# Second layer: where a rounding, an addition and a reciprocal stand among the work of ScalarE and VectorE

## The chip, the cores and the metric

The kernel runs on one core of a Trainium2 chip. TensorE (PE) multiplies matrices, VectorE (DVE) and ScalarE (ACT) do the elementwise work, GpSimd (POOL) a few small powers, and SyncE (SP) starts nearly all the DMAs. Each engine works through its own list of instructions in order and waits for the others through semaphores. The metric is the device time in microseconds (us) of one execution, as the median of several runs.

## The reference

Two layers work on x of shape (4, 512, 256), in float32. Each one normalizes x, computes a mixing branch s and a gated feed-forward branch, and adds their product to x:

```python
x = L0_attn_x
xn = _layernorm(x, axis=-1)
s = _L0_attn_ref(xn, ...)
g = _silu(_L0_ffn_ref(xn, ...))
x = x + s * g
xn = _layernorm(x, axis=-1)
s = _L1_attn_ref(xn, ...)
g = _silu(_L1_ffn_ref(xn, ...))
x = x + s * g
```

The feed-forward branch computes `silu(x @ W1.T) * (x @ W3.T)` with 1024 hidden values, a Walsh-Hadamard transform over them, and a product with W2. The second layer's mixing branch is a causal softmax attention over 512 positions with a second layer norm ahead of it:

```python
scores = jnp.where(causal[None], q @ k.T * scale, -jnp.inf)   # per batch
out = jax.nn.softmax(scores) @ v @ o_proj + residual
```

## The kernel before, in words

The four batches are worked on one after another, first all of layer one, then all of layer two. All products are made from pairs: a value is split into a high half that has been rounded to TensorE's fast format (`split`, line 59: ScalarE rounds, VectorE subtracts) and a low half, and a product is the sum of three matmuls, high by high, high by low and low by high.

In layer two the function `ffn_s` (line 556) handles one batch's feed-forward branch in four steps q = 0 to 3, each with a quarter of the hidden values. The up-projections of a step are done by a Strassen-like scheme of seven products in three PSUM banks: `gate_` (gu…g), `lin` (gu…l) and `z` (gu…z). The order is A11 into `gate_`, S1 into `z`, S2 into `gate_`, S4 into `z`, S3 into `gate_`, A12 into `lin`, A22 into `gate_`. Between them VectorE and ScalarE copy what the banks hold so far: `lin` from `gate_` (line 629), `h1` from `z` (635), `v` from `gate_` (638), then v = z + v (647) and h1 = gate_ + h1 (650). In q = 1 VectorE makes these copies, in other steps ScalarE. Each copy has to be done before TensorE accumulates on in that bank. At the end Silu is applied to h1 and h0 (599), and they are multiplied by v (654) and by `lin` (668), and split (hh and hl, lines 61 and 62). In the trace the tile h carries both h1 and h0.

The attention of the same batch and the down-projection (`behind`) of the step before are laid between these products at eight places per step, through the lists `places`. The order of TensorE's instructions is fixed by hand this way (`line["fixed"]`). The order on VectorE and ScalarE is chosen by the scheduler of the language, unless an `issue_after` (the helper `after`, line 458) puts an instruction behind another. Names that the steps speak of:

- `sc` (line 795): scores of a tile of 128 rows, with mask (812) and row maximum (814), for the tiles 0 to 3.
- `soft` (818): the exponentials (829) of two tiles, each with its sum in `den`. They need another activation table than Silu has, so a table load stands ahead of the first, and another ahead of the next Silu. `first["table"]` keeps the instruction behind which the next one with a table has to stand.
- `pt` (836): transposes of the exponentials on TensorE, then a split of them (ph, pl).
- `pv` (850): product with v; `rden` is the reciprocal of the sums (854), by which line 867 scales the product and adds it to xn.
- `left` in `ffn_s`: the split of h0 of step q = 0 is done in step q = 1, behind the copy of v.
- `gate` (685): for the batch before, g = silu(feed-forward) (692), times s (698), added to x (699), and the store of that half (1039); it is called for half 0 and half 1 by `later_gates` in step q = 1. In batch 0 this was done earlier, for layer one, so no such addition stands there.
- `xt` and `tq`: the next batch's transposed input and its product with the joint query and key weights, in steps 2 and 3.

SP starts, in order, the loads of the next step's weights (`load_s`, line 344), the small round trip through DRAM that spreads the second norm's moments (`there`, `mrb`), and the stores of finished halves.

Of the kernel before, what the change touches and what calls it, by code (L numbers as in the profile page):

```python
# [21 lines left out]
P = 128  # L22
# [13 lines left out]
def kernel(ctx: ExitStack, tc: tile.TileContext, a: dict, out: bass.AP):  # L36
# [7 lines left out]
    def t4(name, shape, dt=F32):  # L44
        return act.tile(shape, dt, tag="t4", name=name, bufs=10)
# [510 lines left out]
    def ffn_s(name, b, pairs, w2, beside, before, last=None):  # L556

        w2h, w2l = w2  # L560
        xh, xl = xTs[1, b]
        outs, dns = {}, []

        def out_of(t):
            if last is not None:
                if t not in outs:
                    outs[t] = psum(f"{name}dn{t}", [P, D], **DN[t // 2])
            elif t not in outs:
                dns.append(psum(f"{name}dn{t // 2}", [P, 2, D], tag="dn", bufs=2))
                outs[t], outs[t + 1] = dns[-1][:, 0, :], dns[-1][:, 1, :]  # L570
            return outs[t]

        def down(q, c, hs, tiles):
            for t in tiles:
                hh, hl = (h[:, c, sl(t % 2)] for h in hs[t // 2])
                o = out_of(t)
                for n, (l, r) in enumerate(((hh, w2h), (hh, w2l), (hl, w2h))):
                    matmul(
                        o, l, r[:, 2 * q + c, :],
                        start=q + c + n == 0 and (t % 2 == 0 or last is not None),  # L580
                        stop=q == NH // 2 - 1 and c == 1 and n == 2,
                        skip_group_check=True,
                    )

        def units(q, hs):

            return [
                lambda c=c, tiles=tiles: down(q, c, hs, tiles) for tiles in ((0, 1), (2, 3)) for c in range(2)
            ]

        def bank(n):
            return psum(f"{name}gu{n}", [P, 2, D], tag="gu", bufs=3)

        def halves(n, dt=F32):
            return hid(f"{name}{n}", dt).rearrange("p (c n) -> p c n", c=2)

        def silu(o, i):
            with after(first["table"]):
                first["table"] = nc.scalar.activation(o, i, AF.Silu)

        hidden, behind, left = {}, before, []
        for q in range(NH // 2):
            wh, wl = pairs(q)
            places = beside[q]

            def place(n):
                for what in places[n]:
                    if isinstance(what, tuple):
                        down(what[0], what[1], hidden[what[0]], what[2])
                    elif isinstance(what, int):  # L610
                        behind[what]()
                    else:
                        what()

            def product(o, i, j, begin=False, end=False):


                for n, (w, x) in enumerate([(wh, xh), (wl, xh), (wh, xl)]):
                    for c in range(2):
                        matmul(  # L620
                            o[:, c, :], w[:, i, sl(c)], x[j],
                            start=begin and n + c == 0, stop=end and n == 2, skip_group_check=True,
                        )

            copy = nc.vector.tensor_copy if q == 1 else nc.scalar.copy
            gate_ = bank(f"{q}g")
            product(gate_, A11, B11, begin=True)
            lin = bank(f"{q}l")
            copy(lin, gate_)
            place(0)  # L630
            place(1)
            z = bank(f"{q}z")
            product(z, S1, T1, begin=True)
            h1, v, h0 = halves(f"h1_{q}"), halves(f"v{q}"), halves(f"h0_{q}")
            copy(h1, z)
            place(2)
            product(gate_, S2, T2)
            copied = copy(v, gate_)
            for what in left:
                with after(copied), after(first["table"]):  # L640
                    what()
            left = []
            place(3)
            product(z, S4, B22, end=True)

            with after(first.pop("scaled", None)):
                nc.vector.tensor_tensor(v, z, v, ALU.add)
            place(4)
            product(gate_, S3, T3)
            nc.vector.tensor_tensor(h1, gate_, h1, ALU.add)  # L650
            place(5)
            product(lin, A12, B21, end=True)
            silu(h1, h1)
            nc.vector.tensor_tensor(h1, h1, v, ALU.mult)
            hs = [(halves(f"hh{i}_{q}", F32R), halves(f"hl{i}_{q}", F32R)) for i in range(2)]
            split(h1, *hs[0])
            place(6)
            product(gate_, A22, T4, end=True)
            hidden[q] = hs
            if last is not None and q == NH // 2 - 1:  # L660

                for c in range(2):
                    silu(h0[:, c, :], gate_[:, c, :])
                    nc.vector.tensor_tensor(h0[:, c, :], h0[:, c, :], lin[:, c, :], ALU.mult)
                    split(h0[:, c, :], *(z[:, c, :] for z in hs[1]))
                break
            silu(h0, gate_)
            first["gate"] = nc.vector.tensor_tensor(h0, h0, lin, ALU.mult)

            left.append(run(split, h0, *hs[1]))  # L670
            if q:
                left.pop()()
            place(7)
            behind = units(q, hs)
        if last is None:
            return behind, dns
        for q, c, t in (
            (2, 0, 2), (2, 1, 2), (2, 0, 3), (2, 1, 3), (3, 0, 0), (3, 1, 0), (3, 0, 1), (3, 1, 1),
            (3, 0, 2), (3, 0, 3), (3, 1, 2), (3, 1, 3),
        ):  # L680
            down(q, c, hidden[q], (t,))
            if (q, c) == (3, 1):
                last(t, outs[t])

    def gate(name, dn, s, x, store=None, halves=range(2)):

        rest = []
        for i in halves:
            ts_ = slice(2 * i, 2 * i + 2)
            g = t2(f"{name}g{i}", [P, 2, D])  # L690
            with after(first["table"]):
                first["table"] = nc.scalar.activation(g, dn[i], AF.Silu)
            rest.append((g, ts_))

        def add():
            for i, (g, ts_) in zip(halves, rest):
                with after(first.get("moments")):
                    nc.vector.tensor_tensor(g, g, s[:, ts_, :], ALU.mult)
                nc.vector.tensor_tensor(x[:, ts_, :], x[:, ts_, :], g, ALU.add)
                if store is not None:  # L700
                    store(i, ts_)

        return add
# [27 lines left out]
    class Attention:  # L731
# [83 lines left out]
                    self.neg[:, t : t + 1], self.scs[t][:, : (t + 1) * P], AX.X, negate=True  # L815
                )

        def soft(self, h):

            b, ins = self.b, first["table"]  # L820
            if h == 0:
                self.ps, self.prs = [], []
            half = t4(f"p{b}_{h}", [P, 2, S])
            for i in (2 * h, 2 * h + 1):
                sc = self.scs[i]
                w = (i + 1) * P
                p = half[:, i % 2, :]
                with after(ins):
                    ins = nc.scalar.activation(
                        p[:, :w], sc[:, :w], AF.Exp,  # L830
                        bias=self.neg[:, i : i + 1], accum_out=self.den[:, i : i + 1],
                    )
                self.ps.append(p)
            first["table"] = ins
# [15 lines left out]
        def pv(self, i):  # L850
            b, xn, pr = self.b, self.xn, self.prs[i]
            if i == 0:
                self.rden = small(f"rden{b}")
                nc.vector.reciprocal(self.rden, self.den)
            if i % 2 == 0:
                self.o = psum(f"pv{b}_{i}", [P, 2, D])
            o = self.o[:, i % 2, :]
# [43 lines left out]
    def run(f, *args):  # L901
        return lambda: f(*args)
# [165 lines left out]
    for b in range(B):  # L1068
        a, final = atts[b], b + 1 == B
        sc, pv, v = ([run(f, i) for i in range(NT)] for f in (a.sc, a.pv, lambda i: a.v(i // 2, i % 2)))  # L1070
        soft = [run(a.soft, i) for i in range(2)]
        pts = [run(a.pt, *tiles) for tiles in ((0, 1), (2,), (3,))]
        adds, later_gates = {}, [lambda: None] * 2
        if b:
# [9 lines left out]
        if not final:  # L1084
            if b == 0:
# [5 lines left out]
            atts.append(c)  # L1091
            places += [
                [
                    [sc[2]], [sc[3], soft[0], rows, soft[1]], [0], [pts[0]],
                    [1, later_gates[0]], [pts[1], later_gates[1]], [2], [pv[0], pv[1], 3],
                ],
                [
# [9 lines left out]
        else:  # L1107
            later = [[(q, c, (2, 3)) for c in range(2)] for q in range(2)]
            places += [
                [[sc[2]], [sc[3], *soft], [0], [pts[0]], [1, later_gates[0]], [pts[1], later_gates[1]], [], [pv[0], pv[1]]],  # L1110
                [[pts[2]], [pv[2], 0], [], [pv[3]], [1], [later[0][0]], [], [later[0][1]]],
                [[later[1][0]], [later[1][1]], [], [0], [], [1], [], []],
            ]
# [69 lines left out]
```

## Time and profile before

| quantity | us |
|---|---|
| median of 3 runs | 361.06 |
| the runs | 361.01 to 361.54 |
| profiled execution, its own time | 361.18 |
| its span in the trace | 359.4 |
| busy: TensorE matmul / weight load | 352.8 / 327.2 |
| busy: VectorE / ScalarE / GpSimd | 287.5 / 197.9 / 20.8 |
| granted TensorE clock | 1.00 |

Layer two fills the trace from about 170 us to the end: the first scores of batch 0 start at 175.6, and step q = 1 of the batches 0 to 3 begins at 180.5, 227.5, 274.4 and 321.4. A line of the timeline gives start, duration, engine, line of the code, operation, what is written and read, and in brackets how long the engine was idle before it and for what. A line of the waits gives who waited for whom, the total, how often, and the longest. Matmuls overlap, so that for TensorE the distance from start to start tells more than the duration.

### The profile page before, as it was taken

The page shows a single profiled execution, that of the slowest core. Times are in us where ns is not written, and L with a number is a line of the kernel's source. Part 1 is how long each engine was busy: PE and PEld are TensorE (multiplying, and loading weights), DVE is VectorE, ACT ScalarE, POOL GpSimd, SP SyncE. Part 2 cuts the span into 40 slices and gives each one's busy share as a digit, 9 for nine tenths or more (in the row PEclk, how much of TensorE's full clock was granted, in tenths as well). Part 3 has the DMA queues.
Part 4 walks back from the last instruction along what each step waited for, and adds up shares of the span by engine and source line. Part 5 has one row for each costly group of instructions (what it writes and reads, how often), then busy time and mean ns, then how long its engine had stood idle before and what let it go on. Part 6 is the DMA issues. An engine that isn't in the chain of part 4 may idle for free.

```text
span 359.4 us, 6279 instructions
## 1 busy us (share of the span) xinstructions
PE 352.8 (98%) x2477; PEld 327.2 (91%) x2477; DVE 287.5 (80%) x597; ACT 197.9 (55%) x373; POOL 20.8 (6%) x22
## 2 busy tenths in 40 slices
PE   8999999999999999999999999999999999999995
PEld 6878988888988898888999999999999999999995
DVE  6899658998579938998987957989679897568646
ACT  4666156265463425664477655576555676556443
POOL 2000110300020110100100001100011000000000
PEclk9999999999999999999999999999999999999999
DMA  7935000301044317656256136652554645345401
GB/s 237 339 102 192 2 1 2 114 3 60 0 168 172 132 44 249 243 181 191 90 216 253 58 148 207 226 208 95 204 193 162 214 169 204 128 159 196 191 2 58
DMA packets 16285, 52.25 MB, mean 145 GB/s; under 512 B 1633, under 2 KB 7937, under 8 KB 16257
## 3 DMA queue, kind: packets, MB, share of 16 engines
q1 hardware_dynamic: 15968, 51.60, 40.6%
q8 instruction: 19, 0.31, 0.4%
q10 hardware_dynamic: 288, 0.26, 0.2%
q14 instruction: 10, 0.07, 0.1%
HBM read 42.40 MB, written 9.45 MB: 144 GB/s over the span
## 4 chain that ended last, share of the span: by engine, by line
PE 85%; DVE 12%; ACT 1%; DMA 1%; POOL 1%; issue 0%; DVEq 0%
PE f_0gu L70 6%; PE f_1gu L70 6%; PE f_2gu L70 6%; PE f_3gu L70 6%; PE f_3dn L70 6%; PE f_2dn L70 6%; PE f_0dn L70 5%; PE f_1dn L70 5%; PE pv L70 4%; PE o L70 3%; PE tq L70 3%; PE v L70 2%; PE sc L70 2%; PE w2ps L70 1%; PE pt L70 1%; DVE neg L814 1%
## 5 line engine op out<-in xcount | busy, mean ns | idle before, releaser
L70 PE MATMUL f_1gu<-xt,w 128*128 128x512 f32 x96 | 24.9, 396 | 0.3 <-ACT xt L61 0.3
L70 PE MATMUL f_3gu<-xt,w 128*128 128x512 f32 x96 | 25.0, 396 | 0.0
L70 PE MATMUL f_2gu<-xt,w 128*128 128x512 f32 x96 | 24.8, 395 | 0.0
L70 PE MATMUL f_0gu<-xt,w 128*128 128x512 f32 (+1 forms) x108 | 24.3, 378 | 0.0
L70 PEld LDWEIGHTS f_0gu<-xt,w 128*128 128x128 f32 x108 | 18.4, 188 | 4.6 <-issue 1.0
L70 PEld LDWEIGHTS f_1gu<-xt,w 128*128 128x128 f32 x96 | 17.0, 188 | 3.7 <-ACT xt L61 0.5
L70 PEld LDWEIGHTS f_2gu<-xt,w 128*128 128x128 f32 x96 | 17.0, 188 | 3.0
L70 PEld LDWEIGHTS f_3gu<-xt,w 128*128 128x128 f32 x96 | 17.0, 188 | 2.9
L61 ACT CAST f_2hh<-f_2h 128x512 fp32r<-128x512 f32 x16 | 9.9, 622 | 15.6 <-DVE f_2h L523 12.5
L70 PE MATMUL f_3dn<-w2l,f_3hh 128*128 128x256 f32 x64 | 17.7, 281 | 0.0
L70 PE MATMUL f_3dn<-w2h,f_3hh 128*128 128x256 f32 x64 | 17.7, 281 | 0.0
L70 PE MATMUL f_1dn<-w2l,f_1hh 128*128 128x256 f32 x64 | 17.7, 281 | 0.0
L70 PE MATMUL f_2dn<-w2h,f_2hh 128*128 128x256 f32 x64 | 17.7, 282 | 0.0
L70 PE MATMUL f_1dn<-w2h,f_1hh 128*128 128x256 f32 x64 | 17.6, 280 | 0.0
L70 PE MATMUL f_2dn<-w2l,f_2hh 128*128 128x256 f32 x64 | 17.6, 280 | 0.0
L70 PE MATMUL f_3dn<-w2h,f_3hl 128*128 128x256 f32 x64 | 17.0, 281 | 0.0
L70 PE MATMUL f_1dn<-w2h,f_1hl 128*128 128x256 f32 x64 | 17.0, 281 | 0.0
L70 PE MATMUL f_2dn<-w2h,f_2hl 128*128 128x256 f32 x64 | 16.7, 281 | 0.0
L61 ACT CAST f_3hh<-f_3h 128x512 fp32r<-128x512 f32 (+1 forms) x17 | 10.0, 595 | 10.1 <-DVE f_3h L523 6.0
L61 ACT CAST f_1hh<-f_1h 128x512 fp32r<-128x512 f32 x16 | 9.9, 622 | 9.7 <-DVE f_1h L523 6.6
L62 DVE TENSOR_TENSOR f_2hl<-f_2h,f_2hh 128x512 fp32r<-128x512 f32 x16 | 10.9, 680 | 3.9 <-ACT f_2hh L61 3.8
L70 PE MATMUL f_0dn<-w2h,f_0hl 128*128 128x256 f32 x48 | 13.7, 284 | 0.1
(487 smaller groups left out, 1146.1 us busy)
## 6 DMA issues: line engine op xcount, KB each, us to landing
sw<-s SPq DMA_DIRECT2D x32, 896.0 KB, 5.4
s<-sp SPq DMA_DIRECT2D x8, 512.0 KB, 4.0
s<-sp SPq DMA_DIRECT2D x8, 384.0 KB, 2.8
w2raw<-in_w SPq DMA_DIRECT2D x4, 512.0 KB, 5.1
sraw<-in_w SPq DMA_DIRECT2D x4, 512.0 KB, 3.3
mrb<-there SPq DMA_DIRECT2D x4, 512.0 KB, 3.7
w13raw<-in_w SPq DMA_DIRECT2D x3, 512.0 KB, 6.1
x<-in_x SPq DMA_DIRECT2D x3, 512.0 KB, 3.5
```

The costliest lines, as they stand in the source:

```text
L61: h = nc.scalar.copy(hi, src)
L62: return h, engine.tensor_tensor(lo, src, hi.bitcast(F32), ALU.subtract)
L70: ins = call(*args, **kwargs)
L814: nc.vector.reduce_max(self.neg[:, t : t + 1], self.scs[t][:, : (t + 1) * P], AX.X, negate=True)
```

## The change

Three orders are changed; nothing is computed otherwise.

- The split of h0 of step 0, done in step 1, now records its rounding as the instruction behind which the next exponential stands. `soft` takes a list of tiles instead of a pair, and the exponential of tile 3 is called on its own, behind that rounding. It was called together with that of tile 2.
- The second half's addition to x in `gate` is put behind the addition of step q = 1 that ends in h1 (line 650). The multiplication by s isn't.
- The reciprocal of the softmax sums is put behind that same addition.

```diff
             for what in left:
                 with after(copied), after(first["table"]):
-                    what()
+                    first["table"] = what()[0]
...
-            nc.vector.tensor_tensor(h1, gate_, h1, ALU.add)
+            first["h1"] = nc.vector.tensor_tensor(h1, gate_, h1, ALU.add)
...
                     nc.vector.tensor_tensor(g, g, s[:, ts_, :], ALU.mult)
-                nc.vector.tensor_tensor(x[:, ts_, :], x[:, ts_, :], g, ALU.add)
+                with after(first.get("h1") if i else None):
+                    nc.vector.tensor_tensor(x[:, ts_, :], x[:, ts_, :], g, ALU.add)
                 if store is not None:
                     store(i, ts_)
...
-        def soft(self, h):
+        def soft(self, *tiles):
...
-            if h == 0:
+            if tiles[0] == 0:
                 self.ps, self.prs = [], []
-            half = t4(f"p{b}_{h}", [P, 2, S])
-            for i in (2 * h, 2 * h + 1):
+            for i in tiles:
+                if i % 2 == 0:
+                    self.half = t4(f"p{b}_{i // 2}", [P, 2, S])
...
-                nc.vector.reciprocal(self.rden, self.den)
+                with after(first["h1"]):
+                    nc.vector.reciprocal(self.rden, self.den)
...
-        soft = [run(a.soft, i) for i in range(2)]
+        soft = [run(a.soft, *tiles) for tiles in ((0, 1), (2,), (3,))]
...
-                    [sc[2]], [sc[3], soft[0], rows, soft[1]], [0], [pts[0]],
+                    [sc[2]], [sc[3], soft[0], rows, soft[1]], [0], [soft[2], pts[0]],
...
-                [[sc[2]], [sc[3], *soft], [0], [pts[0]], [1, later_gates[0]], [pts[1], later_gates[1]], [], [pv[0], pv[1]]],
+                [[sc[2]], [sc[3], *soft[:2]], [0], [soft[2], pts[0]], [1, later_gates[0]], [pts[1], later_gates[1]], [], [pv[0], pv[1]]],
```

More of the change, by code (lines that the diff above doesn't have):

```diff
@@ L816, in sc @@
                 )
-        def soft(self, h):
+        def soft(self, *tiles):
             b, ins = self.b, first["table"]
-            if h == 0:
+            if tiles[0] == 0:
                 self.ps, self.prs = [], []
-            half = t4(f"p{b}_{h}", [P, 2, S])
-            for i in (2 * h, 2 * h + 1):
+            for i in tiles:
+                if i % 2 == 0:
+                    self.half = t4(f"p{b}_{i // 2}", [P, 2, S])
                 sc = self.scs[i]
                 w = (i + 1) * P
-                p = half[:, i % 2, :]
+                p = self.half[:, i % 2, :]
                 with after(ins):
```

## The prediction

> **What bounds the kernel now.** I read the page first: busy shares, then the chain that ended last.
>
> ```profile
> span 359.4 us, 6279 instructions
> PE 352.8 (98%) x2477; PEld 327.2 (91%) x2477; DVE 287.5 (80%) x597; ACT 197.9 (55%) x373; POOL 20.8 (6%) x22
> PE 85%; DVE 12%; ACT 1%; DMA 1%; POOL 1%; issue 0%; DVEq 0%
> ```
>
> TensorE carries the span, so the change is worth only the stalls of TensorE that it removes, less those that it adds. The waits of the weight loader (PEld) from 170 us on, the second layer, list them (us in total, times, longest):
>
> ```profile
> PEld tq L70 <- DVE xgl L62: 0.4, 1, 0.4
> PEld f_2gu1g L70 <- DVE f_2v L638: 0.3, 1, 0.3
> PEld f_1gu1g L70 <- DVE f_1v L638: 0.3, 1, 0.3
> PEld f_0dn L70 <- DVE f_0hl L62: 0.3, 1, 0.3
> PEld f_2gu2z L70 <- issue: 0.2, 1, 0.2
> PEld f_1gu2z L70 <- issue: 0.2, 1, 0.2
> ```
>
> Batches 0, 1 and 2 each have one stall of 0.3 in step q=1, where the change works. Batch 2 in the timeline of all engines (start, duration; later lines are the chain behind the exponentials):
>
> ```profile
> 279.99 0.68 DVE L699 TENSOR_TENSOR x<-x,g_1g 128x512 f32<-128x512 f32 x1
> 280.59 0.68 DVE L814 TENSOR_REDUCE neg<-sc 128x1 f32<-128x512 f32 x1
> 281.19 0.67 DVE L638 COPY f_2v<-f_2gu1g 128x512 f32<-128x512 f32 x1
> 281.92 0.76 PEld L70 LDWEIGHTS f_2gu1g<-tb,sw 128*128 128x128 f32 x6 [0.32 <-DVE f_2v L638]
> ...
> 283.26 0.48 ACT L61 CAST ph<-pt 128x384 fp32r<-128x384 f32 x1 [0.66 <-PE pt L70]
> 283.75 1.28 ACT L599 ACT_TABLE_LOAD   x1
> 285.05 0.63 ACT L599 ACTIVATE f_2h<-f_2h 128x512 f32<-128x512 f32 x1
> 285.71 0.69 DVE L654 TENSOR_TENSOR f_2h<-f_2h,f_2v 128x512 f32<-128x512 f32 x1 [1.05 <-ACT f_2h L599]
> ...
> 287.86 0.68 DVE L668 TENSOR_TENSOR f_2h<-f_2h,f_2gu1l 128x512 f32<-128x512 f32 x1
> ```
>
> The addition to x stands before the copy of v, and product S3 into that bank waits for the copy. The matmul before it started at 281.52 and the usual step is 0.12, so 281.92 is 0.28 late; the product then takes 0.81 to the next start instead of 0.71. The stall costs 0.38. Batch 1 likewise: 234.54 to 234.93, then 0.82: 0.38. Batch 0 waits for the low half of the old gated values: 189.51 to 189.89, then 0.22 to the next instead of 0.12: 0.36. Batch 3, product A22 behind the h1 addition (L650, ends 330.15): 0.86 where that step takes 0.80 in the other batches, then 0.81 for 0.71: 0.16. Together 1.28.
>
> A second gate follows. The first z product of step 2 takes the bank that L668 reads: in batch 2 L668 ends at 288.54 and the product starts at 288.68, in batch 1 at 241.57 and 241.71. Batch 0:
>
> ```profile
> 192.71 0.69 DVE L62 TENSOR_TENSOR f_0hl<-f_0h,f_0hh 128x512 fp32r<-128x512 f32 x1 [0.69 <-ACT f_0hh L61]
> 193.32 0.48 DVE L867 SCALAR_TENSOR_TENSOR xn<-pv,rden,xn 128x256 f32<-128x256 f32 x1
> 193.72 0.68 DVE L668 TENSOR_TENSOR f_0h<-f_0h,f_0gu1l 128x512 f32<-128x512 f32 x1
> 194.31 0.48 DVE L867 SCALAR_TENSOR_TENSOR xn<-pv,rden,xn 128x256 f32<-128x256 f32 x1
> 194.54 0.94 PE L70 MATMUL f_0gu2z<-tb,sw 128*128 128x256 f32 x6
> ```
>
> L668 ends at 194.40, again 0.14 before the product: this gate is just met.
>
> **What the skill says.** Perfetto Trace Analysis, Identifying the Most-Contended Engine: matmul busy share misleads, weight-load busy share is better. The page has 98% and 91%; I count start-to-start steps instead. TensorE: Matmul & The Clock Gate (its table of specifications): VectorE's and ScalarE's queues are strictly first in, first out. That fits: the copy of v started only behind the addition, although its bank was full at 279.94. ScalarE: Activation LUTs, What ACT_TABLE_LOAD costs: 1283 ns and a drain of some 1380 ns. The load is 1.28 here, but the Silu starts 0.02 behind it; no drain shows, so I price a load at 1.28. Perfetto Trace Analysis, Identifying Dependency Chains: an instruction that waits for two engines may get a separate semaphore instruction ahead of it. The z product, which waits for DVE and PE, starts 0.14 after DVE's end, the one-engine waits 0.05 (281.86 to 281.92); the trace doesn't show why.
>
> **The change, step by step.** Nothing is added or removed; TensorE's order stays. As built, ScalarE gets exponential 2, rounding hh, exponential 3; VectorE gets the second addition to x and the reciprocal behind the h1 addition. DVE steps start to start: 0.60 for 128x512, 0.08 for the reciprocal, 0.40 for a gate of pv.
>
> Batches 1 and 2. Without the addition ahead of it, v is copied at 280.59 and ready at 281.27; TensorE comes at 281.64: 0.38 gone. Next in line: pl 281.19, v addition 281.65, hl 282.25 (hh now runs 281.24 to 281.85), h1 addition 282.85 to 283.53. Product A22 needs it at 284.11, the Silu at 284.65: met. Then x 283.45 and reciprocal 284.05, pl 284.13 to 284.67 and the product L654 at 285.33, behind the Silu's end at 285.30. The moved 0.68 is covered by the 1.05 of idle time before L654; without cover it would cost 0.68. The exponential of tile 3 moves from 281.30 to 281.77 and its accumulator is read by 282.55; ScalarE's next work, rounding ph, waits for the transposes until 282.88, 0.38 earlier than before. So table load, Silu, L654, L668 and the z product all come 0.38 earlier. In batch 1 the same sum puts L654 at 238.36 (was 238.74). 0.38 each.
>
> Batch 0 has no x addition. hh runs 187.36 to 187.98, hl ends at 188.76: the stall of 0.36 is gone. But the Silu (190.67) waits for ph and the table load, which that stall didn't delay, so L668 isn't earlier. VectorE's new order puts both gates of pv ahead of it: 192.71 + 0.61 + 0.40 + 0.40 = 194.12, end 194.80, z product 194.94: 0.40 later than 194.54. This delay then meets a wait: tq waits for xgl, which VectorE, busy without a gap from 196.08, finishes at 206.34; tq's two late steps (206.02 to 206.39, 206.39 to 206.73, usual 0.23) cost 0.25. VectorE's chain isn't delayed by as much: its addition at 197.01 then waits for the transposes, which end at 196.63 + 0.40 = 197.03. TensorE arrives at 206.65, after xgl, so the 0.25 goes. Net +0.15. Bounds: 0 (if L668 isn't the gate, TensorE comes early and waits for xgl anyway) and +0.40.
>
> Batch 3. hh 326.06, exponential 3 326.59 to 327.28, ph 327.27; VectorE: hl 327.43, v addition 328.03, pl 328.63, h1 addition 329.31 to 329.99, against TensorE's arrival at 330.15: 0.16 gone. But L668, whose chain doesn't move, ends at 334.76 and lets the z product go at 334.90, where TensorE would come at 334.86. Net -0.12.
>
> DMAs. SP's order stays. The second half's store waits for x: 284.17 in batch 2 (was 281.37, behind mrb), in batch 1 237.17 (236.32), ahead of the next weights (285.15, 238.18); in batch 3 330.63 (324.78), ahead of weights issued at 330.98, which land within 6.4 and are read at 343.0. Five us of slack or more hide it; without that it would cost what the store's issue takes, 0.39.
>
> Sum: 0.15 - 0.38 - 0.38 - 0.12 = -0.73. Profiled time 361.18, span 359.39, so span 358.66; the median shown is 361.06: 360.33.
>
> **Rivals.** *Little comes back* (chance 0.22): batch 0 keeps its 0.40 and batch 3 gains nothing: 0.40 - 0.76 = -0.36, 360.7. For it: the gate of batch 0 is exact. Against: tq's wait of 0.4.
> *Batch 0 is free* (0.22): -0.76 - 0.12 = -0.88, or -0.92 with batch 3's full 0.16: 360.2. For it: in batch 0 TensorE itself reaches the z product at 194.54 (four transposes, 194.10 to 194.54, the same 0.44 as those before them), so L668 may not be the gate there. Against: the 0.14 is the same in all three batches.
> *Slower: the moved addition lands on the Silu path* (0.07). Its place is before pl and L654. If the idle time there were used, 0.68 in batches 1, 2 and 3: -0.73 + 2.04 = +1.31, 362.4. VectorE must reach L654 over 0.63 later than worked out in batches 1 and 2 before it costs anything, and about 1.1 in three batches to make the kernel 0.2% slower. The idle 1.05 speaks against.
> That the edits don't change the order isn't possible as built; that they change it to no effect is the upper end of the first rival.
>
> **How the numbers follow.** 0.2% is 0.72, about what this kernel's measurement can tell from no change. The sum (0.49) has its own range, -0.5 to -1.0, and straddles that bound: 0.3 beyond it. Faster: 0.3 + 0.22 + 0.02 = 0.54; slower 0.06 of the 0.07; the rest, 0.40, same. Range: from 359.9 (second rival, 0.3 to spare) to 360.9 (the first, 0.2 to spare); the slower rival is outside.
>
> **What would show it.** The weight loader's waits lose v in batches 1 and 2 and hl in batch 0, and perhaps tq; they gain the z product of step 2 in batch 0, some 0.7. L668 in batch 0 starts at 194.1 with both gates of pv ahead of it. The idle time before L654 in batches 1 and 2 falls from 1.05 to about 0.65. A z product of batch 0 near 194.5, a wait for h1 before A22, or L654 not following its Silu would prove me wrong.

## The result, and the profile after

The changed kernel takes 360.57 us (median of 22 runs, 360.36 to 360.88), the kernel before 361.21 us (22 runs, 361.01 to 361.62). The ratio is 0.9982, with a 95% interval of 0.9976 to 0.9988: 0.64 us less, between 0.43 and 0.87. That is a gain that the runs tell from nothing, and at 0.18% it lies inside the 0.2% that the prediction named as its bound.

The page after, in the same three lines: span, busy shares, and the chain that ended last by engine.

```profile
span 359.0 us, 6278 instructions
PE 352.4 (98%) x2477; PEld 328.1 (91%) x2477; DVE 287.5 (80%) x597; ACT 197.8 (55%) x373; POOL 20.8 (6%) x22
PE 96%; DVE 2%; ACT 1%; issue 0%; DVEq 0%
```

The busy time of every engine is what it was. VectorE's share of the chain fell from 12% to 2%: the stretches in which the chain ran through VectorE, up to the two late copies of v and the late low half, are out of it (two further 1% shares, of DMA and GpSimd, left the list as well). The waits of the weight loader from 170 us on say the same:

```profile
PEld f_0gu2z L70 <- PE xt_1tp L70: 0.8, 1, 0.8
PEld f_2gu2z L70 <- issue: 0.2, 1, 0.2
PEld f_1gu2z L70 <- issue: 0.2, 1, 0.2
```

The waits for v (twice), for the low half and for xgl are gone, and one of 0.8 is new: the z product of step 2 in batch 0. Batch 2, in the timeline of all engines:

```profile
280.01 0.68 DVE L815 TENSOR_REDUCE neg<-sc 128x1 f32<-128x512 f32 x1
280.61 0.68 DVE L638 COPY f_2v<-f_2gu1g 128x512 f32<-128x512 f32 x1
...
281.66 0.87 PE L70 MATMUL f_2gu1g<-tb,sw 128*128 128x256 f32 x6
...
283.47 0.68 DVE L700 TENSOR_TENSOR x<-x,g_1g 128x512 f32<-128x512 f32 x1
...
285.35 0.69 DVE L654 TENSOR_TENSOR f_2h<-f_2h,f_2v 128x512 f32<-128x512 f32 x1 [0.68 <-ACT f_2h L599]
...
287.50 0.68 DVE L668 TENSOR_TENSOR f_2h<-f_2h,f_2gu1l 128x512 f32<-128x512 f32 x1
```

v is ready at 281.29, TensorE starts at 281.66 without having waited. The addition stands behind h1, and the idle time before L654 has shrunk from 1.05 to 0.68. In this batch the two traces happen to be level in time, so that the starts can be compared with the worked ones directly: v 280.61 (worked 280.59), x 283.47 (283.45), L654 285.35 (285.33), L668 287.50 (worked 287.86 - 0.38 = 287.48).

Batch 0, in the same view:

```profile
193.00 0.69 DVE L62 TENSOR_TENSOR f_0hl<-f_0h,f_0hh 128x512 fp32r<-128x512 f32 x1 [0.69 <-ACT f_0hh L61]
193.61 0.87 DVE L871 SCALAR_TENSOR_TENSOR xn<-pv,rden,xn 128x256 f32<-128x256 f32 x2
194.40 0.68 DVE L668 TENSOR_TENSOR f_0h<-f_0h,f_0gu1l 128x512 f32<-128x512 f32 x1
...
195.22 0.47 PE L70 MATMUL f_0gu2z<-tb,sw 128*128 128x256 f32 x2 [0.59 <-DVE f_0h L668]
```

Both gatings of pv (now line 871) stand ahead of L668, which starts at 194.40 and ends at 195.08; the z product starts 0.14 later. (This trace runs 0.29 behind the one before, see below: 194.40 is 194.11 on that clock, where 194.12 was worked out.) The list of waits above puts the weight loader's 0.8 down to the transposes (xt_1tp). These were done at 194.63, 0.59 before the product started; TensorE's own line names the wait that counts, for L668. The chain that ended last shows where that comes from, in pieces merged by order of time (start, us, what):

```profile
189.17 0.48 ACT ph L61
...
189.66 1.28 ACT L599
...
190.96 0.64 ACT f_0h L599
...
191.62 0.70 DVE f_0h L654
...
193.00 0.69 DVE f_0hl L62
193.69 0.79 DVE xn L871 x2
194.48 0.61 DVE f_0h L668
195.08 0.14 issue
195.22 0.94 PE f_0gu2z L70 x6
```

It is the path of the prediction: rounding of the transposed exponentials, table load, Silu, L654, rounding and low half, two gatings, L668, z product.

The two profiled executions differ from the start: in the one after, the first product of layer one begins 0.33 later, and TensorE is still 0.29 late when it enters step q = 1 of batch 0. The change leaves layer one as it is, and this offset varies from trace to trace (from 0.10 ahead to 0.21 late in the traces of the experiments below). I therefore count each batch from its own entrance, from the starts of TensorE's products in both timelines:

| where | worked | measured |
|---|---|---|
| batch 0, at the z product of step 2 | +0.40 | +0.39 |
| batch 0, behind tq | +0.15 | +0.13 |
| batch 1 | -0.38 | -0.37 |
| batch 2 | -0.38 | -0.37 |
| batch 3 | -0.12 | -0.05 |
| sum | -0.73 | -0.70 (with 0.04 of drift between batches) |

The spans differ by 0.4 (359.4 and 359.0): 0.70 less the late start of 0.29.

### The profile page after: what moved, and what is told of

Read it like the earlier page. It is cut to its first block, busy times and chain, and to the rows that moved or that the text cites. A ratio compares the mean times of both kernels' runs of the same rounds, so it can differ in the third digit from the quotient of the medians.

```text
span 359.0 us, 6278 instructions
## 1 busy us (share of the span) xinstructions
PE 352.4 (98%) x2477; PEld 328.1 (91%) x2477; DVE 287.5 (80%) x597; ACT 197.8 (55%) x373; POOL 20.8 (6%) x22
## 4 chain that ended last, share of the span: by engine, by line
PE 96%; DVE 2%; ACT 1%; issue 0%; DVEq 0%
PE f_1dn L70 6%; PE f_2dn L70 6%; PE f_1gu L70 6%; PE f_0gu L70 6%; PE f_2gu L70 6%; PE f_3gu L70 6%; PE f_3dn L70 6%; PE f_0dn L70 6%; PE sc L70 4%; PE pv L70 4%; PE o L70 3%; PE v L70 3%; PE tq L70 3%; PE warm L70 2%; PE w2ps L70 1%; PE pt L70 1%
## 5 line engine op out<-in xcount | busy, mean ns | idle before, releaser
L70 PE MATMUL f_0dn<-w2l,f_0hh 128*128 128x256 f32 x48 | 13.7, 286 | 0.0
```

What stands on the lines that cost most here:

```text
L70: ins = call(*args, **kwargs)
```

## The experiments

The theory (A) is the one of the prediction: the moved addition gains in batches 1 and 2, the rounding removes a stall of batch 0 that the order of VectorE gives back at L668, and the reciprocal does nothing. The rival (B) is that the rounding is what gains. Each experiment is compared with the kernel before on the same chip (361.24 in the first four, 361.30 in the last three).

**One part at a time.** The rounding alone, made from the changed kernel by taking the other two back:

```diff
-                with after(first.get("h1") if i else None):
-                    nc.vector.tensor_tensor(x[:, ts_, :], x[:, ts_, :], g, ALU.add)
+                nc.vector.tensor_tensor(x[:, ts_, :], x[:, ts_, :], g, ALU.add)
...
-                with after(first["h1"]):
-                    nc.vector.reciprocal(self.rden, self.den)
+                nc.vector.reciprocal(self.rden, self.den)
```

> Only the rounding is put between the last two exponentials; the addition to x and the reciprocal stay as before. Theory A (each stall has the cause that the sum names): batch 0 as in the changed kernel, +0.13 us net (stall of 0.36 gone, z product of step 2 0.4 late, tq's 0.25 gone), batches 1 and 2 keep their stalls of 0.38 behind the copy of v, batch 3 between 0 and -0.05: +0.1 us in all, 361.3. Theory B (the rounding is what gains, by an earlier low half in every batch): -0.5 us or more, and the copy's stalls of batches 1 and 2 gone.

Measured: 361.34 us, ratio 1.0002 (0.9994 to 1.0010). The weight loader's waits in layer two:

```profile
PEld f_0gu2z L70 <- PE xt_1tp L70: 0.8, 1, 0.8
PEld f_2gu1g L70 <- DVE f_2v L638: 0.3, 1, 0.3
PEld f_1gu1g L70 <- DVE f_1v L638: 0.3, 1, 0.3
PEld f_2gu2z L70 <- issue: 0.2, 1, 0.2
PEld f_1gu2z L70 <- issue: 0.2, 1, 0.2
```

Batch 0 is as in the changed kernel, batches 1 and 2 as before. Theory B falls: by itself the rounding gains nothing. Its loss of 0.1 is too small for the times; in the trace, counted from its own entrance, TensorE is 0.40 late at the z product and 0.13 late behind tq. VectorE's new order is shown to come with this edit: here both gatings stand ahead of L668, while with the addition alone or the reciprocal alone (the next two experiments) one stands behind it, as before.

The addition alone, made from the kernel before:

```diff
-            nc.vector.tensor_tensor(h1, gate_, h1, ALU.add)
+            first["h1"] = nc.vector.tensor_tensor(h1, gate_, h1, ALU.add)
...
-                nc.vector.tensor_tensor(x[:, ts_, :], x[:, ts_, :], g, ALU.add)
+                with after(first.get("h1") if i else None):
+                    nc.vector.tensor_tensor(x[:, ts_, :], x[:, ts_, :], g, ALU.add)
```

> Only the second half's addition to x is put behind h1; the rounding and the reciprocal stay as before. Theory A: batches 1 and 2 lose 0.38 us each, batch 3 up to 0.05, and batch 0 stays as it was, with its wait for the low half and its wait of tq: -0.8 us, 360.4, a little less than the whole change. Theory B: no more than 0.2 us is gained.

Measured: 360.43 us, ratio 0.9978 (0.9971 to 0.9985), 0.81 less. The waits are the complement:

```profile
PEld tq L70 <- DVE xgl L62: 0.4, 1, 0.4
PEld f_0dn L70 <- DVE f_0hl L62: 0.3, 1, 0.3
PEld f_2gu2z L70 <- issue: 0.2, 1, 0.2
PEld f_1gu2z L70 <- issue: 0.2, 1, 0.2
```

The gain is the addition's. The whole change (0.9982) is not faster than this part of it. A batch 0 that costs 0.13 would fit, but the two intervals overlap for the most part, so the times alone don't separate them.

The reciprocal alone:

```diff
-                nc.vector.reciprocal(self.rden, self.den)
+                with after(first["h1"]):
+                    nc.vector.reciprocal(self.rden, self.den)
```

> Only the reciprocal is put behind h1. Both theories: nothing; at most the low half in batch 0 comes 0.08 us later, behind the reciprocal, and that stall becomes 0.34 instead of 0.26; tq's wait takes it up. 361.2.

Measured: 361.24 us, ratio 1.0002 (0.9994 to 1.0010): nothing. The wait for the low half in batch 0 reads 0.4 instead of 0.3, and at the z product TensorE is where it was, within 0.03.

**Is L668 the gate?** The waits in the lists say "issue" or name the transposes, so this needed a test that moves L668 and nothing ahead of it on TensorE:

```diff
                 for t in (i - 1, i):
-                    nc.vector.scalar_tensor_tensor(
-                        xn[:, t, :], self.o[:, t % 2, :], self.rden[:, t : t + 1], xn[:, t, :],
-                        ALU.mult, ALU.add,
-                    )
+                    with after(first["gate"] if i == 1 else None):
+                        nc.vector.scalar_tensor_tensor(
+                            xn[:, t, :], self.o[:, t % 2, :], self.rden[:, t : t + 1], xn[:, t, :],
+                            ALU.mult, ALU.add,
+                        )
```

`first["gate"]` is at that point the product by `lin` of the same step.

> The whole change, and in every batch the two gatings of pv for tiles 0 and 1 (line 871) stand behind the product by lin (L668). Theory A (L668 gates the z product of step 2 in all of batches 0 to 2): batch 0's product starts about 0.75 us earlier relative to its predecessors, without a wait; VectorE's chain to tq is earlier too, so batch 0 gives -0.6 instead of +0.13; batches 1 and 2 lose their wait of 0.12 before the z product and the 0.07 behind it: -0.15 each. Against the changed kernel -1.0 us, 359.6. Rival: the z product waits for something else (the transposes ahead of it, the bank's older products), and the time stays within 0.1 us of the changed kernel.

Measured: 359.29 us, ratio 0.9948 (0.9936 to 0.9961): 1.28 less than the changed kernel, where 1.0 was expected. The timeline of batch 0:

```profile
192.88 0.69 DVE L62 TENSOR_TENSOR f_0hl<-f_0h,f_0hh 128x512 fp32r<-128x512 f32 x1 [0.69 <-ACT f_0hh L61]
193.49 0.68 DVE L668 TENSOR_TENSOR f_0h<-f_0h,f_0gu1l 128x512 f32<-128x512 f32 x1
194.08 0.87 DVE L872 SCALAR_TENSOR_TENSOR xn<-pv,rden,xn 128x256 f32<-128x256 f32 x2
194.23 0.78 PEld L70 LDWEIGHTS f_0gu2z<-tb,sw 128*128 128x128 f32 x6
194.26 0.97 PE L70 MATMUL f_0gu2z<-tb,sw 128*128 128x256 f32 x6
```

L668 directly follows the low half, and TensorE no longer waits. The only wait of layer two that is left in the list:

```profile
PEld tq L70 <- DVE xgl L62: 0.2, 1, 0.2
```

Counted as in the table above, batch 0 gives -0.69 against the kernel before, so -0.82 against the changed one (0.73 was expected); the z products of batches 1 and 2 give another -0.2 each and that of batch 3 -0.1, which the expectation left out. So L668 is the gate in batches 0 to 2. Behind it, the two gatings make TensorE wait for nothing: no such wait is in the list.

The experiment also corrects a reading of the prediction. These are the four transposes and the z product behind them in batch 1, in the kernel before (first two lines) and here:

```profile
241.16 0.60 PE L70 MATMUL xt_2tp<-ident,xn 128*128 128x128 f32 x4
241.71 0.95 PE L70 MATMUL f_1gu2z<-tb,sw 128*128 128x256 f32 x6
...
240.29 0.60 PE L70 MATMUL xt_2tp<-ident,xn 128*128 128x128 f32 x4
240.64 0.95 PE L70 MATMUL f_1gu2z<-tb,sw 128*128 128x256 f32 x6
```

From start to start that is 0.55 us before and 0.35 here. In batch 2 it is 0.56 and 0.36, in batch 0 0.44 (194.10 to 194.54) and 0.36. The prediction took 0.44 for TensorE's own pace, so that L668 seemed to be just met in batch 0. In fact L668 already held the product up by some 0.08 there, and by 0.2 in batches 1 and 2, where the expectation above had read 0.12.

**Where that gain lies.** The same edit with the condition `i == 1 and b == 0`, batch 0 alone:

> The whole change, and the two gatings of pv stand behind L668 in batch 0 alone. Theory A: batch 0 as with all gates behind (-0.7 us instead of +0.13), batches 1 and 2 keep the wait of 0.12 before the z product and what follows, 0.2 each: 0.4 us slower than with all gates behind, 359.7. Rival: what the gates gained lies in batches 1 to 3, and this kernel is near the changed one, 360.5.

Measured: 359.84 us, ratio 0.9958 (0.9944 to 0.9972). The gain of batch 0 is there: counted from its own entrance, TensorE is 0.82 earlier behind batch 0 than in the changed kernel, about two thirds of the 1.28. The rest, 0.5 where 0.4 was expected, is in batches 1 to 3; the waits of 0.2 for "issue" in batches 1 and 2 are back in the list.

**What the rounding is worth once L668 is out of the way.** The addition alone, with the gatings behind L668, and rounding and reciprocal as before:

> The addition to x moved and the two gatings of pv behind L668, but the rounding and the reciprocal where they were before. Theory A: the rounding is worth its 0.36 us in batch 0 as soon as L668 no longer takes it back, so that this kernel has the stall of the low half in batch 0 again and is 0.4 us slower than with the rounding, 359.7. Rival: the rounding is worth nothing even then, and the time is 359.3.

Measured: 359.80 us, ratio 0.9958 (0.9945 to 0.9970). With the rounding it was 359.29 on another chip, whose kernel before was 0.06 faster; that leaves 0.45. The two traces say it more closely: counted from its own entrance, TensorE is 0.35 later than with the rounding from this stall on, and 0.37 at the end. The wait that is back, alone in the list:

```profile
PEld f_0dn L70 <- DVE f_0hl L62: 0.3, 1, 0.3
```

So the rounding removes a true stall; in the change as it was made, the order of VectorE in batch 0 took it back. (The reciprocal also differs between these two kernels; by itself it did nothing.)

**Is the moved addition covered?** The changed kernel with more such additions, their results unused, ahead of L654: one in batch 1, three in batch 2.

```diff
+                for n in range({"g1_0": 1, "g1_1": 3}.get(name, 0) if i else 0):
+                    spare = t2(f"{name}again{n}", [P, 2, D])
+                    with after(first["h1"]):
+                        first["again"] = nc.vector.tensor_tensor(spare, g, s[:, ts_, :], ALU.add)
...
-            nc.vector.tensor_tensor(h1, h1, v, ALU.mult)
+            with after(first.pop("again", None)):
+                nc.vector.tensor_tensor(h1, h1, v, ALU.mult)
```

> The whole change, with further additions of the same size between the addition to x and the product L654, their results unused: one in batch 1, three in batch 2. The sum says that the moved addition is covered by idle time of VectorE before L654, of which 0.69 and 0.68 us are left in the changed kernel. Then one addition (0.60) costs nothing in batch 1, and three in batch 2 put L654 1.1 us later and the z product of step 2 by 1.1, or by up to 1.6 since the scheduler then puts another 0.6 ahead of L668: 361.7 to 362.2 in all. Rival (the idle time is not free, because the addition delays something on the way): batch 1 loses 0.6 as well.

Measured: 362.20 us, ratio 1.0026 (1.0016 to 1.0037). VectorE in batch 1 and in batch 2:

```profile
237.75 0.71 DVE L705 TENSOR_TENSOR g_0again<-g_0g,xn 128x512 f32<-128x512 f32 x1
238.57 0.69 DVE L655 TENSOR_TENSOR f_1h<-f_1h,f_1v 128x512 f32<-128x512 f32 x1
...
284.36 2.10 DVE L705 TENSOR_TENSOR g_1again<-g_1g,xn 128x512 f32<-128x512 f32 x3
286.38 0.69 DVE L655 TENSOR_TENSOR f_2h<-f_2h,f_2v 128x512 f32<-128x512 f32 x1
```

L655 here is L654 of the changed kernel. TensorE runs 0.25 ahead of the changed kernel's trace at the z product of batch 0 already, and 0.21 behind L654 in batch 1 and in batch 2 up to the z product, so batch 1 loses nothing: L654 at 238.57, against 238.78 there. In batch 2 it is at 286.38 where 285.14 would be level, 1.24 late, and the z product comes 1.69 late; as expected, a low half of the transposed exponentials (0.60) now stands ahead of L668 too. The room is there, one addition in it is free, and what goes past it delays the z product. The rival of the prediction that ends slower is thus real as a mechanism. Its point of decision is bracketed: one addition is free, and three, which take 2.02 in all, put L654 1.24 late. By that difference the room in batch 2 is about 0.8, a little more than the 0.63 of the prediction.

## Why the prediction was right, point by point

The median fell by 0.64 us where 0.73 was forecast; 360.57 was measured where 360.33 was forecast. The kernel before also read 0.15 higher over more runs (361.21 for 361.06), so most of the gap between the two absolute times is not the sum's.

- **What bounds it.** Right. Only TensorE's stalls counted; all four that the prediction lists are gone from their places, two new waits came at z products (batches 0 and 3), and busy time stayed.
- **Batches 1 and 2.** Right to 0.01 each, and shown by the addition alone (-0.81).
- **Batch 0.** Right: the z product is 0.39 late, and TensorE is 0.13 late behind tq. The step that chose +0.15 between 0 and +0.40, with tq's wait taking up the rest, held: the wait for xgl is gone from the list.
- **Batch 3.** Right in mechanism, too large in size: -0.05 where -0.12 was worked out. The stall at A22 went (its step is 0.80 now). The z product waited for L668, as foreseen, and starts 0.15 after it ends. What the sum left out is that a product that has waited takes longer to the next start: 0.79 here (334.54 to 335.33) against 0.72 before. I had counted that 0.1 for the stalls that go away and not for the one that comes.
- **DMAs.** With the offset of each trace taken off, the stores moved as worked out (284.17 in batch 2, 237.59 in batch 1, 330.25 in batch 3), the next weights were issued at 284.79, 238.22 and 330.73, and no wait for them shows. That the slack hides a later store was read from the traces, not tested by itself.
- **The rivals.** "Little comes back" and "batch 0 is free" are both out: batch 0 gives 0.26 of its 0.39 back at tq. What spoke for the second, that TensorE itself seemed to reach the z product of batch 0 only at 194.54, was the misread step of 0.44 named above. The slower one has its cover, tested above.
- **The chances.** "Faster by over 0.2%" was held likeliest; the measured 0.18% is just on the other side of that line. The sum, 0.73, stood 0.01 beyond the 0.72 of the line, so the side on which the time would fall was a matter of luck, and no part of the mechanism hangs on it.

## What to carry to other kernels

Add up the bounding engine's stalls by start-to-start steps, and then follow each one to the next gate before counting it: a stall that is removed is worth its length only if what waits next comes earlier too. Where an instruction moves on an in-order engine, read the built order of the whole neighbourhood; here a rearrangement that nobody asked for (a second gating ahead of L668) cost 0.40 at the z product, as much as the rounding gained (0.36). And when a removed stall doesn't pay, look for the instruction that frees the next buffer: giving it precedence brought another 1.28 us here, twice the gain of the change itself (359.29 us).

## What the runs showed that I had not expected

- A product that waits for VectorE and for TensorE's own earlier work starts 0.14 to 0.15 us behind VectorE's end in all four batches, one that waits for VectorE alone 0.05. In the records of the first kind a separate semaphore instruction stands ahead of the product's weight load: in batch 1 of the changed kernel L668 ends at 241.60, that instruction runs from 241.64 to 241.69, the weight load starts at 241.72 and the product at 241.75. The second kind has none. That its 0.05 and the steps around it are the whole difference is not tested.
- The additions of the cover experiment stand 0.67 us apart on VectorE (2.02 for three), while the additions of the changed kernel take 0.60 (283.47 to 284.06). What differs isn't shown: these write scratch tiles in a row and read the same two tiles.
- Putting the gatings behind L668 in batches 1 and 2 gave 0.2 each where 0.15 was expected: the whole of it is in the start of the z product, whose wait was 0.2 and not the 0.12 that had been read.
